# The second layer's injections three steps ahead, with the inputs laid two quarters from the step sizes

## The chip, the core and the metric

The kernel runs on one core of a Trainium2 chip. The metric is the time of one execution on the device in microseconds, from repeated runs of the whole kernel. A core has several engines with an instruction stream each, which meet only at semaphores: TensorE (PE in the profile, with its weight loads as PEld) multiplies matrices and writes into PSUM; VectorE (DVE), ScalarE (ACT) and GpSimd (POOL) work on rows of 128 partitions; SyncE (SP) issues the transfers between memories. All data here are float32.

## The reference

The input x has 8 images of 128 channels, 128 x 128 pixels. A first layer (a dilated convolution, Fourier transforms, a gate) makes an image of the same shape from it; the change doesn't touch it. The second layer is a 3 x 3 convolution, then a small state-space scan on each pixel, a group norm, a SiLU and a residual. The scan reads a pixel's 128 channels as a sequence of 8 tokens of 16 values:

```python
seq = y.reshape(B * H * W, 8, 16)                    # 8 tokens
xz = seq @ in_proj.T;  xi, z = split(xz)             # 32 inner channels each
xc = silu(causal_conv1d(xi))
dt, Bm, Cm = split(xc @ x_proj.T)                    # 1, 16 and 16 values per token
dt = softplus(dt * dt_proj_w + dt_proj_b)            # 32 step sizes
h = exp(dt * A) * h + (dt * xc) * Bm                 # 32 x 16 states, token after token
y_t = sum_over_16_states(h * Cm)
ym = (y + D * xc) * silu(z);   out = ym @ out_proj.T
```

Three quantities matter here: the decay exp(dt * A), made from the step sizes dt; the injection (dt * xc) * Bm, made from the inputs u = dt * xc; and the states h.

## The kernel before

Layer 2 works on 256 blocks of four image rows, so N = 512 pixels each. The state of a block lies on partitions as 16 states x 8 channels. The 32 inner channels are four groups of eight, and a tile of [128, 2, 512] holds two groups (GP = 2). The 8 tokens times two pairs of groups give 16 steps: step s is token s // 2 and pair s % 2.

For each step the kernel does this:

- `spreads` (the matmuls have L800 in the profile) takes two things out of the tile `du` on PE. `du` has four quarters of 32 rows, one for each group. `lay_du` puts the group's step sizes into rows 0 to 7 of its quarter and its inputs u into rows 8 to 15 (SP, 16 transfers a block, L774). A matmul of 16 rows spreads the step sizes over 128 partitions times A (tile `da`), another spreads the inputs (tile `ups`). Which quarter a matmul reads also decides which 32 rows of the PE array it takes up. In one call the kernel spreads `da` of step s + 1 and `ups` of step s + 2, which lie in opposite halves of the rows.
- `exps` (ACT, L805) takes the exponential of `da` in PSUM.
- `inject` (DVE, L815) multiplies `ups` by B's row `bb` into a new tile `h`.
- `decay` (DVE, L831 in PSUM, or L829 into `ah` in steps 4, 7 and 10) multiplies `da` by the state of the token before; `add` (DVE, L839, or POOL, L837 in those three steps) adds it to `h`.
- `weigh` (POOL, L845) multiplies `h` by C's row into `hc`; `collect` (PE, L866) sums over the states into `yps`.

Steps 14 and 15, the last token, need no new state: `last_decay` (DVE, L850) multiplies the decay into an `hc` that `weigh` made from the states of steps 12 and 13. The first and last token's own injections go a shorter way through `end_products` (POOL, L822), `ends_sum` (PE, L856) and `ends_inputs` (DVE, L860).

The order of the instructions on each engine is written out by hand: `step(i, s)` for s from 2 to 11 and then `seam(i)`, which ends block i and begins block i + 1. Work of several blocks is mixed there: the convolution of block i + 3 (L134), the projections of blocks i + 2 (`project_x`, L736 and ACT L738; `project_z`, L745 and ACT L747) and i + 1 (dt, B and C), the output of block i - 1 (`gated` L877, `project_out` L885, and `keep`, which takes its statistics on DVE, L897, and stores it). Each queue works in that order, so an instruction that waits holds what is behind it.

PSUM has room for one `ups` tile, two `da` tiles (which `project_x` and `project_z` also take in turn), one `pm` for all else and one `yps`. So the spread of an `ups` waits until `inject` has read the one before, and the spread of a `da` until the last reader of the one before the last is through. The pool of `h` tiles has six buffers, that of `du` two.

The middle of a step is, on PE, the spreads; on DVE, decay, add and inject:

```python
spreads([(i, s + 1)], [(i, s + 2)])
exps(i, s + 1)
...
if now:
    decay(i, s)
    if s != 4:
        add(i, s)
    inject(i, s + 2)
```

So at the end of step 11 the injections of block i are made up to step 13, and the seam makes those of steps 0 to 3 of the next block.

Of the kernel before, what the change touches and what calls it, by code (L numbers as in the profile page):

```python
# [26 lines left out]
DI = 32  # L27
DS = 16
KC = 4
NG = 4  # L30
# [559 lines left out]
def layer1(ctx, tc, x1, w1, c1, out):  # L590
# [12 lines left out]
    nc = tc.nc  # L603
# [9 lines left out]
    def cf(name):  # L613
        at, n = C1[name]
        return ct[:, at:at + n]
# [21 lines left out]
    taps = cf("taps").rearrange("p (k l) -> p k l", l=L)  # L637
    w_k = wf("conv1d_w").rearrange("p (k d) -> p k d", d=DI)
    with tc.tile_pool(name="l1_prep", bufs=2) as prep:
# [18 lines left out]
        for hf in range(NH):  # L658
            for l in range(L):
                k = hf * L + l  # L660
# [16 lines left out]
    GP = 2  # L677
# [1 line left out]
    wk1 = ctx.enter_context(tc.tile_pool(name="l1_w1", bufs=1))  # L679
    wk2 = ctx.enter_context(tc.tile_pool(name="l1_w2", bufs=2))  # L680
    wk3 = ctx.enter_context(tc.tile_pool(name="l1_w3", bufs=3))
    hp = ctx.enter_context(tc.tile_pool(name="l1_h", bufs=6))
    hcp = ctx.enter_context(tc.tile_pool(name="l1_hc", bufs=7))
    p_u = ctx.enter_context(tc.tile_pool(name="l1_pu", bufs=1, space=PSUM))
    p_a = ctx.enter_context(tc.tile_pool(name="l1_pa", bufs=2, space=PSUM))
# [10 lines left out]
    def live(i):  # L696
        return 0 <= i < nb
# [4 lines left out]
    def load(i):  # L702
        b, r = blocks[i]
        if r % CH == 0:
            lo, hi = max(0, r - 1), min(H, r + CH + 1)
            xin = wk2.tile([P, CH + 2, W], F32, name="xin")
            nc.sync.dma_start(xin[:, :hi - lo, :], x1[b][:, lo:hi, :])
            xins[b, r // CH] = xin, lo
        st8[i]["xin"] = xins[b, r // CH]
# [20 lines left out]
    def pair():  # L730
        return p_a.tile([P, GP, N], F32, name="da")
# [17 lines left out]
    def project_dt(i, hf):  # L749
        d, pool = st8[i], wk2 if hf else wk1  # L750
        ps = misc().rearrange("p a b -> p (a b)")
        nc.tensor.matmul(ps, m_dtf, d["xc"][:, hf, :], start=True, stop=True)  # L752
        d["dt", hf] = pool.tile([P, N], F32, name=f"dt{hf}")
        nc.scalar.activation(d["dt", hf], ps, AF.Softplus, bias=wf("dt_b"))  # L754
# [12 lines left out]

    def lay_du(i, hf):

        d = st8[i]  # L770
        du = wk2.tile([P, LP, N], F32, name="du")
        for q in range(NG):
            for k, v in ((0, d["dt", hf]), (8, d["u", hf])):
                nc.sync.dma_start(du[q * DI + k:q * DI + k + 8], v[q * DI:(q + 1) * DI, :])  # L774
        d["du", hf] = du

    def lay_states(i, hf, k):
# [9 lines left out]
    def spreads(das, upss):  # L787

        todo = []
        for m, name, k0, steps in ((m_a, "da", 0, das), (m_u, "ups", 0, upss)):  # L790
            for i, s in steps:
                if not live(i):
                    continue
                d, t, k = st8[i], s // GP, s % GP
                d[name, s] = pair() if name == "da" else p_u.tile([P, GP, N], F32, name="ups")
                for q in range(GP):
                    a = (k * GP + q) * 32
                    todo.append((d[name, s][:, q], m[a:a + 16, :], d["du", t // LP][a:a + 16, t % LP, :]))
        for o, w, v in todo:
            nc.tensor.matmul(o, w, v, start=True, stop=True)  # L800

    def exps(i, s):
        if live(i):
            da = st8[i]["da", s]
            nc.scalar.activation(da, da, AF.Exp)  # L805

    def state_row(i, name, t):
        return st8[i][name, t // LP][:, t % LP:t % LP + 1, :].broadcast_to([P, GP, N])

    def inject(i, s):  # L810
        if not live(i):
            return
        d = st8[i]
        h = hp.tile([P, GP, N], F32, name="h")
        nc.vector.tensor_mul(h, d["ups", s], state_row(i, "bb", s // GP))  # L815
        d["h", s] = h
# [24 lines left out]
    def weigh(i, s, t):  # L841

        d = st8[i]
        hc = hcp.tile([P, GP, N], F32, name="hc")
        nc.gpsimd.tensor_mul(hc, d["h", s], state_row(i, "cc", t))  # L845
        d["hc", t * GP + s % GP] = hc

    def last_decay(i, s):
        d = st8[i]
        nc.vector.tensor_mul(d["hc", s], d["da", s], d["hc", s])  # L850
# [11 lines left out]
    def collect(i, t):  # L862

        d = st8[i]
        for g in range(NG):
            nc.tensor.matmul(  # L866
                d["yps"][g * DI:(g + 1) * DI], gather[:, t % LP, :], d["hc", GP * t + g // GP][:, g % GP],
                start=False, stop=(t in (3, 6)), skip_group_check=True)

    def skip(i, hf):  # L870
        d = st8[i]
        nc.tensor.matmul(d["yps"], m_d, d["xc"][:, hf, :], start=False, stop=False, skip_group_check=True)  # L872
# [72 lines left out]
    def step(i, s):  # L945

        now, nxt = live(i), live(i + 1)
        if s == 2:
            if live(i + 4):
                load(i + 4)  # L950
            if live(i - 2) and blocks[i - 2][1] + RB == H:
                norm_of(blocks[i - 2][0])
        spreads([(i, s + 1)], [(i, s + 2)])
        exps(i, s + 1)

        if s == 2:
            if nxt:
                project_dt(i + 1, 0)
            if live(i - 1):
                collect(i - 1, 7)  # L960
        elif s == 3:
            if live(i - 1):
                collect(i - 1, 6)
                skip(i - 1, 1)
            if nxt:
                project_bc(i + 1, 0)
        elif s == 4 and nxt:
            project_dt(i + 1, 1)
        elif s == 5:
            if now:  # L970
                ends_sum(i, 0)
            if nxt:
                project_bc(i + 1, 1)
        elif s == 6:
            if now:
                skip(i, 0)
            if live(i - 1):
                project_out(i - 1, 0, 4)
        elif s == 7 and now:
            collect(i, 1)  # L980
        elif s == 8 and live(i - 1):
            project_out(i - 1, 4, 8)
        elif s == 9 and now:
            collect(i, 2)
        elif s == 11 and now:
            collect(i, 3)
        if s in CONV and live(i + 3):
            conv(i + 3, *CONV[s])

        if now:  # L990
            decay(i, s)
            if s != 4:
                add(i, s)
            inject(i, s + 2)
            if s == 5:
                ends_inputs(i, 0)
            if s == 11:
                gated(i, 0)
        if s == 3 and live(i - 1):
            gated(i - 1, 1)  # L1000

        if now:
            if s == 2:
                end_products(i, 0)
            else:
                weigh(i, s - 1, (s - 1) // GP)
            if s == 4:
                add(i, s)
            if s == 7:
                end_products(i, 1)  # L1010
        if s in (3, 4) and nxt:
            inputs(i + 1, s - 3)
        if s == 9 and "active" in fin:
            last_sum()

        if s == 3 and now:
            lay_states(i, 1, 1)
        elif s == 6 and nxt:
            lay_du(i + 1, 0)
            lay_states(i + 1, 0, 0)  # L1020
        elif s == 8 and tails:
            last_load()
        elif s == 10 and nxt:
            lay_states(i + 1, 0, 1)

    def seam(i):


        now, nxt = live(i), live(i + 1)

        def taps(k0, k1):
            if live(i + 3):
                conv(i + 3, k0, k1)

        spreads([(i, 13)], [(i + 1, 0)])
        exps(i, 13)
        if now:
            ends_sum(i, 1)
            decay(i, 12)
            add(i, 12)  # L1040
            weigh(i, 11, 5)
            weigh(i, 12, 7)
        if nxt:
            lay_states(i + 1, 1, 0)
        taps(5, 6)
        if "loaded" in fin:
            last_act()
        if live(i + 2):
            project_x(i + 2)
        if now:  # L1050
            decay(i, 13)
            add(i, 13)
            weigh(i, 13, 7)
        inject(i + 1, 0)
        if live(i + 2):
            project_z(i + 2)
        spreads([(i, 14)], [(i + 1, 1)])
        exps(i, 14)
        if now:
            ends_inputs(i, 1)  # L1060
        inject(i + 1, 1)
        taps(6, 8)
        spreads([(i, 15)], [(i + 1, 2)])
        exps(i, 15)
        if live(i - 1):
            keep(i - 1)
        inject(i + 1, 2)
        if now:
            collect(i, 4)
            last_decay(i, 14)  # L1070
        taps(8, 9)
        if now:
            weigh(i, 12, 6)
            last_decay(i, 15)
        spreads([(i + 1, 2)], [(i + 1, 3)])
        exps(i + 1, 2)
        inject(i + 1, 3)
        if now:
            collect(i, 5)
            weigh(i, 13, 6)  # L1080
        if live(i + 3):
            turn(i + 3)
        if nxt:
            lay_du(i + 1, 1)
# [95 lines left out]
```

## Time and profile before

| | |
|---|---|
| median of 3 runs | 14885.76 us (14885.24 to 14897.25) |
| the profiled execution | 14897.05 us, its span 14895.3 us |
| first `inject` of layer 2 | at 2070.6 us |
| last `inject` of layer 2 | at 14742.5 us |
| one block of layer 2 (from an inject of the seam to the same one of the next block) | 49.23 us |
| in that block: busy PE, DVE, POOL, ACT | 47.74, 46.42, 45.71, 29.00 us |
| DMA engines' busy share in it | 0.66 |
| mean granted TensorE clock | 0.987 |

A timeline line has the start in us, the duration in us, the engine, the line of the kernel, the operation, the tile written and the tiles read with their shapes, and how many instructions of the kind follow each other; in brackets the engine's idle time ahead of it and what ended that. "issue" there means that the profile shows nothing that it waited for. Durations of neighbours on one engine overlap by up to a tenth of a microsecond, so starts are the better measure. A float32 matmul appears as two instructions. A matmul that takes up only some rows of the array can run beside another one in other rows.

### The profile page before, as it was taken

What the parts mean: (1) busy time and instruction counts of PE and PEld (TensorE: products, weight loads), DVE (VectorE), ACT (ScalarE), POOL (GpSimd) and SP (SyncE); (2) the same over time, 40 slices, a digit from 0 to 9 for tenths busy, and PEclk for the clock granted to TensorE, in tenths of its full rate; (3) what the DMA queues carried; (4) which work ended last, traced back from release to release, by engine and by line L of the source; (5) the groups of instructions that cost most, each with busy time, mean ns of one, the idle gap of its engine ahead of it and who ended that gap; (6) DMA issues with size and microseconds to landing.
All of it is one profiled execution on the core that took longest, in us unless ns stands there. A gap on an engine that the chain in (4) does not pass through costs nothing.

```text
span 14895.3 us, 200912 instructions
## 1 busy us (share of the span) xinstructions
PE 14287.1 (96%) x70696; PEld 5588.1 (38%) x70696; DVE 12683.2 (85%) x12417; ACT 8294.9 (56%) x9234; POOL 12983.2 (87%) x7076
## 2 busy tenths in 40 slices
PE   9999999999999999999999999999999999999996
PEld 6677653333333333333333333333333333333331
DVE  3343359999999999999999999999999999999995
ACT  3354355555555555565655555555555555555553
POOL 6666668989999999999999999999999999999996
PEclk9999999999999999999999999999999999999997
DMA  4444456666666666666666666666666666666665
GB/s 136 139 139 122 129 124 117 120 118 121 130 137 134 137 132 136 133 135 134 135 136 133 136 133 137 133 138 131 137 133 136 132 137 133 134 135 135 136 133 140
DMA packets 1091885, 1976.01 MB, mean 133 GB/s; under 512 B 125760, under 2 KB 256832, under 8 KB 1082688
## 3 DMA queue, kind: packets, MB, share of 16 engines
q1 hardware_dynamic: 1090304, 1960.82, 61.0%
q8 instruction: 563, 9.22, 0.3%
q14 instruction: 442, 3.62, 0.1%
q10 hardware_dynamic: 576, 2.35, 0.0%
HBM read 419.16 MB, written 201.33 MB: 42 GB/s over the span
## 4 chain that ended last, share of the span: by engine, by line
PE 72%; DVE 18%; issue 4%; ACT 4%; DMA 1%; POOL 0%; SPq 0%; DVEq 0%; POOLq 0%; ACTq 0%
PE da L800 19%; PE yps L866 9%; PE ups L800 7%; PE pm L134 7%; DVE da L831 6%; PE m L280 4%; DVE h L839 4%; DVE h L815 4%; PE yps L872 4%; PE pm L752 4%; PE pm L885 3%; PE pm L764 3%; DVE hc L850 2%; PE da L745 2%; PE yps L856 2%
## 5 line engine op out<-in xcount | busy, mean ns | idle before, releaser
L845 POOL TENSOR_TENSOR hc<-h,cc 128x1024 f32<-128x1024 f32 x3584 | 8377.2, 2370 | 427.6 <-DVE h L839 408.5
L805 ACT ACTIVATE da<-da 128x1024 f32<-128x1024 f32 x3584 | 3618.7, 1010 | 4193.3 <-PE ups L800 2491.7
L815 DVE TENSOR_TENSOR h<-ups,bb 128x1024 f32<-128x1024 f32 x3584 | 4368.7, 1219 | 690.1 <-PE ups L800 313.9
L800 PE MATMUL da<-du,m_a 16*128 16x512 f32 x14336 | 4068.1, 644 | 140.5 <-DVE hc L850 135.1
L800 PE MATMUL ups<-du,m_u 16*128 16x512 f32 x14336 | 4114.3, 642 | 2.5 <-DVE h L815 1.4
L839 DVE TENSOR_TENSOR h<-da,h 128x1024 f32<-128x1024 f32 x2304 | 2821.2, 1224 | 79.1
L831 DVE TENSOR_TENSOR da<-da,h 128x1024 f32<-128x1024 f32 x2304 | 2820.1, 1224 | 6.8 <-ACT da L805 3.3
L134 PE MATMUL pm<-xin,l_wt 128*128 128x508 f32 (+1 forms) x4608 | 2412.7, 624 | 177.0 <-ACT xr L890 170.2
L837 POOL TENSOR_TENSOR h<-ah,h 128x1024 f32<-128x1024 f32 x768 | 1818.8, 2368 | 451.2 <-DVE ah L829 409.6
L800 PEld LDWEIGHTS da<-du,m_a 16*128 16x128 f32 x14336 | 1078.4, 184 | 2624.6 <-issue 1002.7
L866 PE MATMUL yps<-hc,l_ct 128*32 128x512 f32 x14336 | 1931.7, 611 | 0.0
L134 PEld LDWEIGHTS pm<-xin,l_wt 128*128 128x128 f32 x4608 | 751.7, 189 | 1620.7 <-issue 1396.0
L800 PEld LDWEIGHTS ups<-du,m_u 16*128 16x128 f32 x14336 | 1124.4, 184 | 380.8 <-DVE h L815 298.2
L805 ACT ACT_TABLE_LOAD x774 | 993.0, 1283 | 30.1 <-PE ups L800 1.3
L829 DVE TENSOR_TENSOR ah<-da,h 128x1024 f32<-128x1024 f32 x768 | 933.1, 1215 | 0.0
L759 POOL TENSOR_TENSOR u<-dt,xc 128x512 f32<-128x512 f32 x512 | 656.0, 1281 | 190.2 <-ACT dt L754 190.2
L866 PEld LDWEIGHTS yps<-hc,l_ct 128*32 128x32 f32 x14336 | 283.6, 108 | 1375.1 <-issue 968.6
L754 ACT ACT_TABLE_LOAD x511 | 655.6, 1283 | 29.6 <-PE pm L752 2.1
L822 POOL TENSOR_TENSOR cb<-bb,cc 128x512 f32<-128x512 f32 x512 | 658.3, 1286 | 11.8 <-DMA cc<-bc 11.8
L885 PEld LDWEIGHTS pm<-m_o,ym 128*128 128x128 f32 x4096 | 517.6, 191 | 317.2 <-issue 316.5
L850 DVE TENSOR_TENSOR hc<-da,hc 128x1024 f32<-128x1024 f32 x512 | 600.6, 1215 | 0.9 <-ACT da L805 0.8
L872 PE MATMUL yps<-xc,m_d 128*128 128x512 f32 x1024 | 584.6, 653 | 0.0
(180 smaller groups left out, 14537.5 us busy)
## 6 DMA issues: line engine op xcount, KB each, us to landing
bb<-bc SPq DMA_DIRECT2D x2048, 256.0 KB
cc<-bc SPq DMA_DIRECT2D x2048, 256.0 KB
du<-dt SPq DMA_DIRECT2D x2048, 64.0 KB
du<-u SPq DMA_DIRECT2D x2048, 64.0 KB
xin<-x SPq DMA_DIRECT2D x152, 768.0 KB
xin<-x SPq DMA_DIRECT2D x112, 640.0 KB
gn<-xr SPq DMA_DIRECT2D x256, 256.0 KB
v<-gn SPq DMA_DIRECT2D x256, 256.0 KB
```

Source lines behind the costliest of these rows:

```text
L134: nc.tensor.matmul(out[:, a:b, wa:wb], wt[:, t, :], src[:, r + dy + a - base:r + dy + b - base, wa + dx:wb + dx], start=(n == 0), stop=(n ...
L800: nc.tensor.matmul(o, w, v, start=True, stop=True)
L805: nc.scalar.activation(da, da, AF.Exp)
L815: nc.vector.tensor_mul(h, d["ups", s], state_row(i, "bb", s // GP))
L829: nc.vector.tensor_mul(d["ah"], da, before)
L831: nc.vector.tensor_mul(da, da, before)
L837: nc.gpsimd.tensor_add(h, d["ah"], h)
L839: nc.vector.tensor_add(h, d["da", s], h)
L845: nc.gpsimd.tensor_mul(hc, d["h", s], state_row(i, "cc", t))
L866: nc.tensor.matmul(d["yps"][g * DI:(g + 1) * DI], gather[:, t % LP, :], d["hc", GP * t + g // GP][:, g % GP], start=False, stop=(t in (3, ...
L872: nc.tensor.matmul(d["yps"], m_d, d["xc"][:, hf, :], start=False, stop=False, skip_group_check=True)
L885: nc.tensor.matmul(d["pm"][:, j, :], d["ym", hf][:, j * C:(j + 1) * C], m_of[:, hf, :], start=(hf == 0), stop=(hf == NH - 1))
```

## The change

It does four things in layer 2. `spreads` and `inject` are given `ups` of step s + 3 beside `da` of step s + 1, instead of s + 2; in step 11 that is step 0 of the next block, and the seam then makes steps 1 to 4. The inputs of a group are laid into the quarter two further on than its step sizes, and the `ups` matmuls read them from there. The pool of `h` has seven buffers. In the seam, `keep` stands ahead of `inject` of step 2, `weigh(i, 12, 6)` ahead of the injection that follows, and the injection of step 3 between the two last decays rather than behind both.

```diff
-    hp = ctx.enter_context(tc.tile_pool(name="l1_h", bufs=6))
+    hp = ctx.enter_context(tc.tile_pool(name="l1_h", bufs=7))
...
         for q in range(NG):
-            for k, v in ((0, d["dt", hf]), (8, d["u", hf])):
-                nc.sync.dma_start(du[q * DI + k:q * DI + k + 8], v[q * DI:(q + 1) * DI, :])
+            for k, v, g in ((0, d["dt", hf], q), (8, d["u", hf], (q + GP) % NG)):
+                nc.sync.dma_start(du[q * DI + k:q * DI + k + 8], v[g * DI:(g + 1) * DI, :])
...
                 for q in range(GP):
-                    a = (k * GP + q) * 32
+                    a = (k * GP + q + (GP if name == "ups" else 0)) % NG * 32
...
-        spreads([(i, s + 1)], [(i, s + 2)])
+        ahead = (i, s + 3) if s < 11 else (i + 1, 0)
+        spreads([(i, s + 1)], [ahead])
...
             if s != 4:
                 add(i, s)
-            inject(i, s + 2)
+        inject(*ahead)
+        if now:
...
-        spreads([(i, 13)], [(i + 1, 0)])
+        spreads([(i, 13)], [(i + 1, 1)])
...
-        inject(i + 1, 0)
+        inject(i + 1, 1)
         if live(i + 2):
             project_z(i + 2)
-        spreads([(i, 14)], [(i + 1, 1)])
+        spreads([(i, 14)], [(i + 1, 2)])
         exps(i, 14)
         if now:
             ends_inputs(i, 1)
-        inject(i + 1, 1)
-        taps(6, 8)
-        spreads([(i, 15)], [(i + 1, 2)])
-        exps(i, 15)
         if live(i - 1):
             keep(i - 1)
         inject(i + 1, 2)
+        taps(6, 8)
+        spreads([(i, 15)], [(i + 1, 3)])
+        exps(i, 15)
         if now:
             collect(i, 4)
             last_decay(i, 14)
+            weigh(i, 12, 6)
+        inject(i + 1, 3)
         taps(8, 9)
         if now:
-            weigh(i, 12, 6)
             last_decay(i, 15)
-        spreads([(i + 1, 2)], [(i + 1, 3)])
+        spreads([(i + 1, 2)], [(i + 1, 4)])
         exps(i + 1, 2)
-        inject(i + 1, 3)
+        inject(i + 1, 4)
         if now:
             collect(i, 5)
             weigh(i, 13, 6)
```

## The prediction

> **What bounds the kernel now.** I read the page first: shares by engine, then slices. Layer 2 fills slices 6 to 40, and three engines are nearly full there.
>
> ```profile
> span 14895.3 us, 200912 instructions
> PE 14287.1 (96%) x70696; PEld 5588.1 (38%) x70696; DVE 12683.2 (85%) x12417; ACT 8294.9 (56%) x9234; POOL 12983.2 (87%) x7076
> L815 DVE TENSOR_TENSOR h<-ups,bb 128x1024 f32<-128x1024 f32 x3584 | 4368.7, 1219 | 690.1 <-PE ups L800 313.9 <-issue 311.2 <-POOL hc L845 38.0
> ```
>
> The groups come next. L815 is `inject`, the product with B. It is the only frequent DVE row with much idle time ahead of it: 690.1 us. The timelines say where. One block takes 49.23 us (the inject at 8015.68 us returns at 8064.91). DVE's gaps per block are 0.80, 1.15, 0.16, 0.16 and 0.22 us, sum 2.49, and all stand before an inject. The first three lie in the seam. With x' for step x of the next block, DVE's seam reads add 13, inject 0', ends_inputs, inject 1', bn_stats, inject 2', last decays 14 and 15, inject 3':
>
> ```profile
> 8011.92 1.22 DVE L839 TENSOR_TENSOR h<-da,h 128x1024 f32<-128x1024 f32 x1
> 8013.06 1.21 DVE L815 TENSOR_TENSOR h<-ups,bb 128x1024 f32<-128x1024 f32 x1
> 8014.19 0.69 DVE L860 TENSOR_TENSOR yps<-yps,u 128x512 f32<-128x512 f32 x1
> 8015.68 1.23 DVE L815 TENSOR_TENSOR h<-ups,bb 128x1024 f32<-128x1024 f32 x1 [0.80 <-PE ups L800]
> 8016.82 0.68 DVE L897 BATCH_NORM_STATS2 st<-xr 128x6 f32<-128x512 f32 x1
> 8018.66 1.22 DVE L815 TENSOR_TENSOR h<-ups,bb 128x1024 f32<-128x1024 f32 x1 [1.15 <-issue]
> 8019.80 2.35 DVE L850 TENSOR_TENSOR hc<-da,hc 128x1024 f32<-128x1024 f32 x2
> 8022.30 1.23 DVE L815 TENSOR_TENSOR h<-ups,bb 128x1024 f32<-128x1024 f32 x1 [0.16 <-PE ups L800]
> ```
>
> Each of those injects starts 0.10 to 0.16 us after its spread on PE. PE's timeline of the same stretch:
>
> ```profile
> 8014.90 0.63 PE L800 MATMUL ups<-du,m_u 16*128 16x512 f32 x2
> 8017.91 0.59 PE L800 MATMUL ups<-du,m_u 16*128 16x512 f32 x2
> 8019.43 1.12 PE L134 MATMUL pm<-xin,l_wt 128*128 128x508 f32 x2
> 8021.07 0.70 PE L800 MATMUL da<-du,m_a 16*128 16x512 f32 x2 [0.52 <-DVE hc L850]
> 8021.61 0.59 PE L800 MATMUL ups<-du,m_u 16*128 16x512 f32 x2
> ```
>
> The reader is to see a chain through both engines. The spread of 2' ends at 8018.50; inject 2' runs from 8018.66; last decay 14 from 8019.80; it frees the PSUM buffer that the spread of da 2' needs; PE, free about 8020.5, sits until 8021.07; its group ends at 8022.20 and inject 3' follows at 8022.30. From there DVE runs without a gap to 8042.6. The chain of waits names the same stations.
>
> **What the Trainium skill says.** "PSUM — Partial Sum Buffer", section "Engine vs sequencer instructions": VectorE's queue is strict FIFO, and matmuls start and complete in program order. The trace agrees: the last decays sat behind inject 2' although nothing of theirs was missing. "TensorE: Matmul & The Clock Gate", "Part 3: Packing small matmuls", "The mechanism": weight loads overlap running matmuls only where the row group differs. The trace shows da and ups groups starting 0.01 us apart and done in about 1.07 us (8008.23 to 8009.30), but 2.26 us where ups had to wait (8040.23 to 8042.49). "ScalarE: Activation LUTs", "What ACT_TABLE_LOAD costs", states 1283 ns; the trace has 1.28 us, and the exp after it starts 1.29 us after the load did, so the further drain that the page counts is not seen here. "Perfetto Trace Analysis", "Identifying the Most-Contended Engine": matmul busy share is no measure of PE's limit. The trace agrees: 1.07 against 2.26 us both count as busy.
>
> **The change part by part.** No instruction is added or removed; 14 injects, 14 da groups and 14 ups groups a block remain.
>
> *Edits that cost nothing.* A seventh h buffer is memory alone. `lay_du` issues the same 16 transfers of 64 KB a block in the same SP order from other rows. With ups three ahead, ups and da of a step have the same parity s; without the shift by two quarters they would share row groups, and a group would take about 2.3 us (1.13 + 1.20, the serial case above) instead of 1.07. With the shift they stay apart: 1.07 stays. In steps 2 to 11 DVE, PE, ACT, POOL and SP keep their order; only the index of ups and inject moves on. So the 0.16 and 0.22 us gaps of steps 7 and 10 stay.
>
> *Inputs needed earlier.* The spread of 0' moves from 8008.24 to the group at 8004.28, inject 0' from 8013.06 to 8006.54. In the second half, ups 8' moves from 8037.12 to 8033.59. du's last transfers are issued at 8042.97 (first half, next block) and 8024.19. The DMA activity in 0.5 us slices from 8037 on, then from 8018 on:
>
> ```profile
> DMA  0000302415545555999989999889887881006889
> DMA  9895554123223314959999998988994400000000
> ```
>
> In the first, the engines are empty from 8054.0 to 8055.0, so B's rows are in before inject 0' (8055.77 for that block); du, issued while the share was at most half, was out ten microseconds before its group at 8053.51. In the second they are mostly idle from 8021.5 to 8026 while du is issued, and everything is in by 8034; du precedes the large transfer behind it, so I put it near 8027, six microseconds early. Cost zero; if that cover failed, each microsecond late would cost up to 255 us in all.
>
> *The seam.* DVE's new order is add 13, inject 1', ends_inputs, bn_stats, inject 2', last decay 14, inject 3', last decay 15, inject 4'. The starts, with durations and start-to-start steps of the rows above (inject to next 1.14, last decay 1.17):
> - inject 1' at 8013.06: its spread is PE's group of 8008.23, done at 8009.37. ends_inputs 8014.19, bn_stats 8014.89 to 8015.57.
> - inject 2': its spread is the group of 8014.35, held there as before by the Silu of xc (ACT, ends 8014.15), done 8015.53, so 8015.68. The 0.80 us gap shrinks to 0.1.
> - last decay 14 needs exp 14, and it now stands ahead of inject 3'. On ACT:
>
> ```profile
> 8014.46 1.02 ACT L747 ACTIVATE zs<-da 128x1024 f32<-128x1024 f32 x1 [0.31 <-PE da L745]
> 8015.56 1.28 ACT L805 ACT_TABLE_LOAD   x1
> 8016.85 1.01 ACT L805 ACTIVATE da<-da 128x1024 f32<-128x1024 f32 x1
> ```
>
>  exp 14 ends at 8017.86, whatever DVE does; with 0.1 us to get across, last decay 14 starts at 8017.96, where DVE has sat since 8016.82: a new gap of 1.1 us takes the place of the 1.15.
> - inject 3': spread done 8018.50; DVE free at 8017.96 + 1.17 = 8019.13, ends 8020.35. last decay 15 at 8020.27 (exp 15 was done at 8019.60, POOL's product for it about 8019.0).
> - PE's group da 2' + ups 4': PE is free at 19.43 + 1.05 = 8020.48; da's buffer is free since 8019.2; inject 3' has freed ups's at 8020.35. It starts 8020.48, not 8021.07, and ends 8021.61.
> - inject 4' at 8021.72 (DVE free at 8021.44), where inject 3' stood at 8022.30.
>
> Gain 0.58 us a block, bounded above by PE's 8020.48. The gaps become 0.1 + 1.1 + 0.3 + 0.38 = 1.9 us against 2.49, which fits. What follows moves along: turn on PE starts at 22.6 instead of 23.14, the next group 23.15 instead of 23.72, exp 2' ends 8022.68 for decay 2' at 8022.86. POOL's long run of products ends near 8024.8 and then waits 1.33 us for add 2'; 0.75 of that is left, so POOL is not reached. bn_stats moved forward costs its 0.68 us in a gap.
>
> *The sum.* 255 seams x 0.57 us (a little off for the exp's crossing, which the trace of before doesn't show by itself: 0.05 to 0.25 us; above about 0.15 the margin before 8020.48 is used up, and at 0.25 the gain is 0.48) = 145 us. The profiled execution took 14897.05 us (span 14895.3 and 1.75 around it), so 14752 for it; the median of the runs, 11 us lower, becomes 14741.
>
> **The rivals.**
> - *Nothing comes of it.* The new wait on exp 14 swallows the gain: last decay 14 at 8018.5 instead of 8017.96 makes inject 4' 8022.3 again. For it: ACT's table load stands right ahead. Against it: exp 14's time is read from the trace and its inputs don't move. Time 14886; so would a change that another engine's cycle takes back at once.
> - *Slower.* The same place, beyond its turning point. DVE's queue is in order, so behind last decay 14 stand inject 3', last decay 15 and inject 4', and PE's group of 2' waits for inject 3' with collect, turn and the next block's projections behind it. It decides from a start at 8018.55; each further 0.1 us costs 26 us. A start at 8018.9, as when the Silu pair on ACT comes 0.9 us later, gives 0.35 x 255 = +89: 14975. Against: xc and z are released by adds 12 and 13, which stand unmoved.
> - *Far faster.* If both gaps went in full (1.95 us), 255 x 1.95 = 497: 14389. exp 14 speaks against all of it; half, were the da chain on PE also early, gives 14640.
>
> **How the numbers follow.** Forecast (14710 to 14800) 0.66; part of it (14800 to 14856) 0.09; nothing 0.09; slower 0.12; far faster 0.04. I take 0.2%, 30 us, as what a measurement of this kernel can tell from no change. Faster 0.79, same 0.09, slower 0.12. The range 14705 to 14870 leaves out far faster, slower and half of nothing, about 0.2.
>
> **What would show it.** Right: block period 48.65 us; DVE's seam gaps near 0.1, 1.1 before a last decay (put down to ACT), 0.3; PE's 0.52 us gap before da gone; L815's idle down by some 400 us and L850's up by 280; da and ups still 0.01 us apart. Wrong: an inject waiting for a DMA, ups groups of 2 us everywhere, last decay 14 later than 0.7 us after exp 14, or POOL without idle time after the seam.

## The result, and the profile after

| | before | after |
|---|---|---|
| median of 4 runs | 14890.93 us (14885.24 to 14897.25) | 14715.84 us (14712.15 to 14717.42) |
| profiled execution, its span | 14897.05, 14895.3 us | 14712.15, 14710.4 us |
| one block of layer 2, median of 255 | 49.233 us | 48.557 us |
| one block, mean of 255 (from one `keep` statistic to the next) | 49.315 us | 48.633 us |
| mean granted TensorE clock | 0.987 | 0.988 |

The ratio is 0.9882 (95% interval 0.9865 to 0.9899): 175 us faster. The mean block is 0.682 us shorter; over 255 blocks that is 174 of the 185 us between the two spans. Of the rest, 3 us lie in layer 1, which the change doesn't touch (the first inject of layer 2 stands at 2067.6 instead of 2070.6 us), about 7 us at the entry to layer 2 and 1 us behind the last statistic.

The page of the changed kernel, in the lines that answer to those of before. In this kernel every line number of the scan is one higher, so `inject` is L816 and `last_decay` L851.

```profile
span 14710.4 us, 200914 instructions
PE 14255.2 (97%) x70696; PEld 5593.5 (38%) x70696; DVE 12679.2 (86%) x12417; ACT 8295.0 (56%) x9234; POOL 12984.8 (88%) x7076
L816 DVE TENSOR_TENSOR h<-ups,bb 128x1024 f32<-128x1024 f32 x3584 | 4362.1, 1217 | 239.6 <-PE ups L801 164.6
L851 DVE TENSOR_TENSOR hc<-da,hc 128x1024 f32<-128x1024 f32 x512 | 623.8, 1218 | 281.2 <-ACT da L806 280.3
```

The busy times are what they were: PE 14287.1 to 14255.2, DVE 12683.2 to 12679.2 us. The idle ahead of `inject` fell from 690.1 to 239.6 us, and 281.2 us of a new wait, on the exp, stand ahead of `last_decay`. The difference, 169 us, is nearly the whole change of time. The seam on DVE, from add 13 to decay 2' (a prime marks a step of the next block):

```profile
8018.82 1.22 DVE L840 TENSOR_TENSOR h<-da,h 128x1024 f32<-128x1024 f32 x1
8019.96 1.21 DVE L816 TENSOR_TENSOR h<-ups,bb 128x1024 f32<-128x1024 f32 x1
8021.10 0.69 DVE L861 TENSOR_TENSOR yps<-yps,u 128x512 f32<-128x512 f32 x1
8021.69 0.68 DVE L898 BATCH_NORM_STATS2 st<-xr 128x6 f32<-128x512 f32 x1
8022.54 1.23 DVE L816 TENSOR_TENSOR h<-ups,bb 128x1024 f32<-128x1024 f32 x1 [0.17 <-issue]
8024.86 1.22 DVE L851 TENSOR_TENSOR hc<-da,hc 128x1024 f32<-128x1024 f32 x1 [1.10 <-ACT da L806]
8026.01 1.21 DVE L816 TENSOR_TENSOR h<-ups,bb 128x1024 f32<-128x1024 f32 x1
8027.14 1.21 DVE L851 TENSOR_TENSOR hc<-da,hc 128x1024 f32<-128x1024 f32 x1
8028.58 1.23 DVE L816 TENSOR_TENSOR h<-ups,bb 128x1024 f32<-128x1024 f32 x1 [0.23 <-PE ups L801]
8029.72 1.22 DVE L832 TENSOR_TENSOR da<-da,h 128x1024 f32<-128x1024 f32 x1
```

Three gaps are left: 0.17, 1.10 and 0.23 us, where there were 0.80, 1.15 and 0.16. Last decay 14 now waits for the exp; inject 3' follows it without a gap. PE in the same stretch:

```profile
8024.78 0.59 PE L801 MATMUL ups<-du,m_u 16*128 16x512 f32 x2
8025.30 1.07 PE L867 MATMUL yps<-hc,l_ct 128*32 128x512 f32 x8
8026.30 1.12 PE L134 MATMUL pm<-xin,l_wt 128*128 128x508 f32 x2
8027.35 0.70 PE L801 MATMUL da<-du,m_a 16*128 16x512 f32 x2
8027.89 0.59 PE L801 MATMUL ups<-du,m_u 16*128 16x512 f32 x2
```

The spread of da 2' starts when the convolution ahead of it is through; the 0.52 us in which it waited for last decay 14 are gone. The list of waits (who waited for whom: us in all, times, longest) says the same of all blocks. In the kernel before, PE's weight loads for da waited 343.9 us, 255 times, for the last decays:

```profile
PEld da L800 <- DVE hc L850: 343.9, 255, 2.4
```

In the changed kernel that wait is gone, and the last decays wait for the exp instead:

```profile
DVE hc L851 <- ACT da L806: 280.3, 255, 1.4
PEld da L801 <- DVE hc L851: 1.1, 1, 1.1
PE da L801 <- DVE hc L851: 0.2, 1, 0.2
```

### The profile page after: what moved, and what is told of

The parts are those of the page before. It is cut to its first block, busy times and chain, and to the rows that moved or that the text cites. A ratio compares the mean times of both kernels' runs of the same rounds, so it can differ in the third digit from the quotient of the medians.

```text
span 14710.4 us, 200914 instructions
## 1 busy us (share of the span) xinstructions
PE 14255.2 (97%) x70696; PEld 5593.5 (38%) x70696; DVE 12679.2 (86%) x12417; ACT 8295.0 (56%) x9234; POOL 12984.8 (88%) x7076
## 5 line engine op out<-in xcount | busy, mean ns | idle before, releaser
L816 DVE TENSOR_TENSOR h<-ups,bb 128x1024 f32<-128x1024 f32 x3584 | 4362.1, 1217 | 239.6 <-PE ups L801 164.6
L851 DVE TENSOR_TENSOR hc<-da,hc 128x1024 f32<-128x1024 f32 x512 | 623.8, 1218 | 281.2 <-ACT da L806 280.3
L752 PE MATMUL pm<-xc,m_dt 128*128 128x512 f32 x1024 | 584.7, 653 | 1.5 <-issue 0.8
```

## The experiments

The theory: the gain comes from the order in the seam, because last decay 14 frees the buffer of da 2' early and inject 3' no longer waits behind both last decays; the exp of step 14 then sets the place of last decay 14, with 0.13 us of margin ahead of PE's own time. The rivals: the earlier injections (three steps ahead) carry it, or the moved statistics do. Except where "before" is named, each edit is made to the changed kernel. Ratios are to the kernel before.

**The order alone**, in the kernel before (two ahead, own quarters, six buffers):

```diff
+        if live(i - 1):
+            keep(i - 1)
         inject(i + 1, 1)
...
-        if live(i - 1):
-            keep(i - 1)
-        inject(i + 1, 2)
         if now:
...
             last_decay(i, 14)
+            weigh(i, 12, 6)
+        inject(i + 1, 2)
         taps(8, 9)
         if now:
-            weigh(i, 12, 6)
             last_decay(i, 15)
```

> The seam's new order alone on the kernel before: two steps ahead, inputs in their own quarters, six h buffers; the statistics stand ahead of the injection of step 1, that of step 2 between the two last decays. Theory (the order of the seam is what gained, because PE's group no longer waits for last decay 14 behind a late injection): about 0.62 us of the 0.68 us a block, 14891 - 255 x 0.62 = 14733 us, ratio about 0.989, block 48.6 us. Rival (it is the third step of distance that gained): ratio 0.998 to 1.0, 14860 to 14890 us.

Measured: 14740.62 us (14722.55 to 14743.53), ratio 0.9898 (0.9883 to 0.9913), block 48.642 us. In the median of its blocks, DVE's seam waits 1.06 us for the exp ahead of last decay 14, and 0.21 and 0.27 us ahead of the injects of 1' and 3'.

**All of the change but the order**: three ahead, the laying and the seventh buffer, with the seam in the old order.

> Three steps ahead, the layout and the seventh buffer, with the seam in the order of before (each injection where its predecessor stood). Theory: only the 0.06 us a block that the body gained is left, 14891 - 15 = 14876 us, ratio 0.998 to 1.0, gaps of 0.80, 1.15 and 0.16 us in the seam again. Rival: 14716 us or near it, ratio 0.988.

Measured: 14866.5 us (14853.76 to 14873.6), ratio 0.9984 (0.9977 to 0.9990), block 49.154 us. The order carries some 150 us, the rest of the change some 25; together they make the 175 measured.

**Last decay 14 put behind inject 3'**:

```diff
             collect(i, 4)
-            last_decay(i, 14)
             weigh(i, 12, 6)
         inject(i + 1, 3)
         taps(8, 9)
         if now:
+            last_decay(i, 14)
             last_decay(i, 15)
```

> The changed kernel with last decay 14 put behind the injection of step 3, next to last decay 15. Theory: PE's group for da of step 2 waits for last decay 14 again (a gap of about 0.5 us ahead of it), nearly the whole gain goes: 14716 + 255 x 0.55 = 14856 us, ratio to before 0.996 to 1.0. Rival (the statistics moved forward made the gain): it stays near 14716 us.

Measured: 14868.27 us, ratio 0.9984 (0.9978 to 0.9991), block 49.154 us. In its DVE timeline one gap of 1.77 us stands where the change has 1.10:

```profile
8003.84 1.23 DVE L816 TENSOR_TENSOR h<-ups,bb 128x1024 f32<-128x1024 f32 x1 [1.77 <-PE ups L801]
8004.98 2.35 DVE L851 TENSOR_TENSOR hc<-da,hc 128x1024 f32<-128x1024 f32 x2
8007.49 1.22 DVE L816 TENSOR_TENSOR h<-ups,bb 128x1024 f32<-128x1024 f32 x1 [0.16 <-PE ups L801]
```

And in its list of waits PE's wait for the last decays is back, once in every block:

```profile
PEld da L801 <- DVE hc L851: 347.2, 255, 2.4
PE da L801 <- DVE hc L851: 138.2, 255, 1.4
```

This one line of order is worth 152 us. It takes away nothing that DVE does; it decides when PE gets its buffer. The theory's chain holds.

**The statistics back** behind inject 2':

```diff
-        if live(i - 1):
-            keep(i - 1)
         inject(i + 1, 2)
...
         exps(i, 15)
+        if live(i - 1):
+            keep(i - 1)
         if now:
```

> The changed kernel with the statistics of keep behind the injection of step 2, where they stood before. Theory: they fall into the 1.1 us in which DVE waits for exp 14, so nothing changes: 14716 us within 15. Rival (moving them forward filled the 0.80 us gap and that was the gain): about 0.6 us a block lost, 14870 us.

Measured: 14717.36 us (14714.02 to 14719.01), ratio 0.9884 (0.987 to 0.9899), block 48.556 us: the time of the change. The gaps become 0.76 us ahead of inject 2' and 0.50 ahead of last decay 14, 1.26 us as against 1.27. The 0.68 us of statistics fill one hole or the other, since last decay 14 can't start before the exp either way. So the smaller gap ahead of inject 2', the one that looks like the gain in the timeline, is worth nothing.

**The exp later.** Three small copies on ACT, whose result nothing uses, stand ahead of the exp of step 14:

```diff
+        if live(i + 2):
+            for k in range(3):
+                nc.scalar.copy(idle, st8[i + 2]["yT"][:, k * P:(k + 1) * P])
```

> The changed kernel with three small copies (128 x 128, results unused) on ACT ahead of exp 14, which makes it later by d, about 0.6 us. Theory: last decay 14 stands ahead of the injection of step 3, so the delay passes on less the margin of about 0.13 us: 14716 + 255 x (d - 0.13), 14836 us for d = 0.6, last decay 14 still within 0.1 us of exp 14. Rival (PE's own work sets the end of the seam and DVE has room): under 14750 us.

Measured: 14896.42 us (14891.36 to 14900.05), ratio 1.0001 (0.9992 to 1.001), block 49.219 us. The whole gain is gone. ACT and then DVE in its timeline:

```profile
8009.90 0.95 ACT L1065 COPY idle<-yT 128x128 f32<-128x128 f32 x3
8010.87 1.28 ACT L808 ACT_TABLE_LOAD   x1
8012.16 1.93 ACT L808 ACTIVATE da<-da 128x1024 f32<-128x1024 f32 x2
```

```profile
8013.27 1.23 DVE L853 TENSOR_TENSOR hc<-da,hc 128x1024 f32<-128x1024 f32 x1 [1.88 <-ACT da L808]
```

The wait grew from 1.10 to 1.88 us. Measured from the end of the activation ahead of it, the exp came 0.79 us later, the block grew by 0.66: the first 0.13 us cost nothing (by the whole time, 181 us or 0.71 us a block, it was 0.08). That is about the margin that the prediction had worked out, and it is why the change doesn't gain more: past it, the exp of step 14 sets the end of the seam.

**Six buffers of h instead of seven**, and the same with an unused tile in the room of the seventh, so that the addresses stay as they are:

```diff
-    hp = ctx.enter_context(tc.tile_pool(name="l1_h", bufs=7))
+    hp = ctx.enter_context(tc.tile_pool(name="l1_h", bufs=6))
```

> The changed kernel with six h buffers. Theory: the nearest reuse is the injection of step 4 (at 8028.58 us in the profile) behind the product of POOL with the states of step 12 (ends about 8028.3), so no wait is added: 14716 us within 20. Rival (three steps ahead needs the seventh buffer): DVE waits for POOL in the seam, 0.2 us a block or more, over 14765 us.

> Six h buffers and an unused tile of the seventh's size in its place (zeroed once, about 1 us), so that every later tile lies at the address that it has in the changed kernel. If the 36 us that six buffers cost come from the waits on the buffers: 14752 us again, injections starting 0.1 us or more after their spread in step 7. If they come from where the tiles lie: 14717 us.

Measured: 14751.76 us (14745.27 to 14754.72), ratio 0.9904 (0.9889 to 0.9919), block 48.673 us; with the unused tile 14747.82 us (14745.47 to 14749.83), ratio 0.9905 (0.989 to 0.992), block 48.673 us. The expectation missed: six buffers were expected to be enough, and the loss of the seventh costs 36 us. No run with six buffers comes within 27 us of a run of the change. The second kernel shows that the place in memory isn't the cause. In the timeline of the first, the injections of step 7 and of 4' start 0.05 us later after their spreads than in the change (gaps of 0.10 and 0.23 us there):

```profile
8016.27 1.23 DVE L816 TENSOR_TENSOR h<-ups,bb 128x1024 f32<-128x1024 f32 x1 [0.15 <-issue]
8044.66 1.22 DVE L816 TENSOR_TENSOR h<-ups,bb 128x1024 f32<-128x1024 f32 x1 [0.28 <-issue]
```

Two times 0.05 us is most of the block's 0.116. The label "issue" alone doesn't rule out a buffer that comes free late, since the inject of 2' in the kernel before has it too and waited for its spread. But in the median the product of POOL that read the buffer last ended 3.7 us (step 7) and 0.46 us (4') before these injects start. What differs stands in the instruction records of the traces: with six buffers these two carry a wait for POOL's semaphore, with seven one for PE's alone. In every run's trace, nearly all injects behind a gap start 0.10 to 0.16 us after the end of their spread where they carry POOL's wait, and 0.04 to 0.10 us where they don't. So a wait that was met long before seems to cost some 0.05 us by being there; no run varies it by itself.

**The order and the seventh buffer**, two ahead, in the kernel before:

> The seam's new order with two steps ahead, the inputs in their own quarters, and seven h buffers: the whole change without its third step of distance. If the seventh buffer is what lies between the order alone (14741 us) and the changed kernel (14716 us), as the 36 us lost with six buffers suggest: 14705 to 14720 us, block 48.53 us or so. If the distance is: 14741 us again, block 48.64 us.

Measured: 14730.26 us (14726.05 to 14736.77), ratio 0.9893 (0.9876 to 0.9909), block 48.587 us. With the runs above, all in the new order:

| | six buffers | seven buffers |
|---|---|---|
| two ahead, own quarters | 14740.62 us, block 48.642 | 14730.26 us, block 48.587 |
| three ahead, shifted quarters | 14751.76 us, block 48.673 | 14715.84 us, block 48.557 |

The 25 us that the order leaves to the rest of the change aren't the distance by itself: with six buffers three ahead was no faster than two (11 us slower, within what these runs can tell). The intervals of the ratios overlap, so how the 25 us divide between distance and buffer stays open; the block periods, in one execution each, put it at 0.03 us for the distance with seven buffers.

**Own quarters with three ahead**:

```diff
-            for k, v, g in ((0, d["dt", hf], q), (8, d["u", hf], (q + GP) % NG)):
+            for k, v, g in ((0, d["dt", hf], q), (8, d["u", hf], q)):
...
-                    a = (k * GP + q + (GP if name == "ups" else 0)) % NG * 32
+                    a = (k * GP + q) * 32
```

> The changed kernel with the inputs left in their own quarter, so that da and ups of one step take up the same rows of the array. Theory: each of the 14 groups takes about 2.3 us in place of 1.07; PE's work, 44.0 us a block when nothing waits (49.23 less 1.49 idle and about 3.7 of groups stretched by waits), becomes 61.6, PE alone sets the period and the time is 14716 + 255 x (61.6 - 48.55) = 18040 us (17000 to 19000). Rival (the groups are mostly stretched by waits anyway, so the rows matter little): under 15000 us.

Measured: 17267.76 us, ratio 1.1594 (1.157 to 1.1617), block 57.0 us, clock 0.963. In PE's timeline the two spreads of a group run one after the other:

```profile
8006.49 1.13 PE L801 MATMUL da<-du,m_a 16*128 16x512 f32 x4
8007.45 1.02 PE L801 MATMUL ups<-du,m_u 16*128 16x512 f32 x4
8008.40 1.06 PE L867 MATMUL yps<-hc,l_ct 128*32 128x512 f32 x8
```

From start to start that is 0.96 + 0.95 = 1.91 us a group instead of 1.07. The direction was as expected, the price 1.91 rather than 2.3 us. The 0.84 us don't count fourteen times, though. In the block of the change looked at, eight of the fourteen groups have their two spreads 0.01 us apart; in the other six the spread of ups waits for the inject that frees its tile, in one of them so long that the group is serial already:

```profile
8046.51 1.13 PE L801 MATMUL da<-du,m_a 16*128 16x512 f32 x4
8047.64 1.13 PE L801 MATMUL ups<-du,m_u 16*128 16x512 f32 x4
```

All fourteen groups of a block, each up to the next matmul on PE, take 18.2 us in the change and 26.8 here: 8.6 us more, and the median block is 8.4 longer. The whole time lost 2552 us, some 400 more than 255 such blocks. The clock fits that: in layer 2 it was granted at half for 1031 us, against 140 in the change, and half of the difference, some 450 us, is an estimate of what that cost. The laying is what three ahead can't do without; alone it was not tried.

**Collect 2 moved** from step 9 to step 8, into PE's wait of 0.68 us there:

```diff
-        elif s == 8 and live(i - 1):
-            project_out(i - 1, 4, 8)
-        elif s == 9 and now:
-            collect(i, 2)
+        elif s == 8:
+            if live(i - 1):
+                project_out(i - 1, 4, 8)
+            if now:
+                collect(i, 2)
```

> The changed kernel with the collect of token 2 on PE moved from step 9 to step 8, ahead of the convolution tap that waits 0.68 us for ACT's copy of the output. Theory: PE reaches the group of step 10 about 0.7 us earlier, DVE's gap of 0.23 us ahead of its injection goes: 14716 - 255 x 0.23 = 14657 us, ratio to before 0.984. Rival (the seam takes it back, or the later group of step 9 holds DVE): 14716 us or slower.

Measured: 14714.98 us (14714.36 to 14715.3), ratio 0.988 (0.9865 to 0.9894), block 48.50 us: the median block is 0.06 us shorter in the profiled execution, the mean block 0.02 at most, and the whole time is that of the change. DVE's gap in step 10:

```profile
8008.93 1.23 DVE L816 TENSOR_TENSOR h<-ups,bb 128x1024 f32<-128x1024 f32 x1 [0.17 <-PE ups L801]
```

It shrank from 0.23 to 0.17 us and no more, since there is one `ups` tile: the spread can start only once the inject before has read it, and takes 1.13 us. A PE that is free earlier has nothing to write into.

**Decay 13 into SBUF** (`ah`), added from there on DVE, which would free a `da` buffer 1.2 us earlier for PE; and the same with collect 2 moved and one convolution tap drawn from step 11 to step 10:

```diff
-        if s in ON_POOL:
+        if s in ON_POOL or s == 13:
             d["ah"] = wk1.tile([P, GP, N], F32, name="ah")
             nc.vector.tensor_mul(d["ah"], da, before)
...
+        elif s == 13:
+            nc.vector.tensor_add(h, d["ah"], h)
```

> The changed kernel with the product of decay 13 written to SBUF in place of PSUM (DVE adds from there), so that the PSUM buffer of da 13 is free for project_z one add (1.25 us) earlier. Theory (PE's chain from z to the group of step 2 sets the end of the seam; x before z ends on PE 0.23 us before z starts now): the gap of 0.23 us ahead of z goes, 14716 - 255 x 0.23 = 14657 us, and no more, since PE itself is then full. Rival (DVE's own order sets the end): 14716 us.

> As in the run before it, and PE's work ahead of the seam moved: the collect of token 2 into the gap of step 8, one convolution tap from step 11 to step 10. Theory: PE reaches the seam's first group about 0.45 us earlier, x then waits only for add 12, z starts 0.58 us earlier than in the changed kernel: 14716 - 255 x (0.58 + 0.06) = 14553 us, ratio to before 0.977. Rival (the tap holds up the group of step 11, or exp 14 holds the seam): 14640 us or slower.

Measured: 15763.98 us (15619 to 15886), ratio 1.0555 (1.0504 to 1.0606), clock 0.953; and 15366.98 us (15314 to 15438), ratio 1.0309 (1.0285 to 1.0333), clock 0.962. Both missed by far. DVE and POOL in the first one's timeline:

```profile
3027.79 4.62 DVE L840 TENSOR_TENSOR h<-ah,h 128x1024 f32<-128x1024 f32 x1
```

```profile
3022.04 9.29 POOL L848 TENSOR_TENSOR hc<-h,cc 128x1024 f32<-128x1024 f32 x4
3032.56 4.64 POOL L848 TENSOR_TENSOR hc<-h,cc 128x1024 f32<-128x1024 f32 x2 [1.23 <-DVE h L840]
```

The add took 4.62 us in place of 1.22. It was issued while POOL ran four products without a pause, and ended at 3032.41, 1.1 us after POOL's last one (3022.04 + 9.29 = 3031.33): in this block it hardly ran at all until POOL stopped.

It isn't so in every block. The median over the 256 blocks, 3.165 us, lies between two outcomes. In 115 blocks the add took 1.2 or 1.3 us, and the product of POOL beside it 3.35 us instead of 2.36. In 124 it took 4.2 us or more, in 102 of these 5.8 or 5.9, held past the ends of two of POOL's products until POOL stopped. What decides between them isn't shown: in those 115 and those 102 blocks alike it was issued 0.13 to 0.23 us before the end of a product of POOL. The Trainium skill, "SBUF — State Buffer", section "Who interferes with whom", says that a VectorE instruction with both inputs in SBUF contends with a GpSimd instruction that reads SBUF, and one with at most one SBUF input, outside the two-port modes, doesn't. This agrees: either the add or POOL's product lost time, while every other product and add of DVE in layer 2 on tiles of this size has one operand in PSUM and keeps its 1.22 us.

What followed cost more. A block with an add of 5.8 us or more lasted 57.3 us in the mean, one with an add under 1.4 us 48.8 us. The median of the latter is 48.53 us, 0.03 below the change, so the 0.23 us that the earlier buffer was to bring didn't show there either. In the second kernel 80 blocks had an add of over 4 us, and the median of the undisturbed ones was 48.53 us again.

In PE's timeline of the first kernel, and in the view of stretches (us, then busy time of PE, PEld, DVE, ACT and POOL, the granted clock, the DMA share, GB/s):

```profile
3030.15 1.13 PE L801 MATMUL da<-du,m_a 16*128 16x512 f32 x4
3033.60 2.07 PE L801 MATMUL ups<-du,m_u 16*128 16x512 f32 x4 [2.33 <-DVE h L816]
3035.61 3.66 PE L134 MATMUL pm<-xin,l_wt 128*128 128x508 f32 x4
```

```profile
3026.50:3029.50 3.00, 3.00 (x10) 1.06 (x8) 2.97 (x3) 1.68 (x2) 3.00 (x3) 1.00 0.97 176
3029.50:3033.00 3.50, 1.63 (x8) 0.30 (x4) 3.50 (x2) 3.21 (x4) 2.27 (x2) 0.89 0.66 166
3033.00:3036.00 3.00, 2.40 (x5) 0.90 (x6) 1.97 (x4) 0.66 (x1) 3.00 (x2) 0.50 0.01 3
3036.00:3039.20 3.20, 3.20 (x5) 0.78 (x4) 2.13 (x2) 0.00 (x0) 1.20 (x1) 0.53 0.00 0
```

PE sat idle for 2.33 us. Within that gap, at about 3032.2, its granted clock fell to half, where it stayed until about 3039: the four convolution matmuls took 3.66 us, as against 1.97 in the change, and what stands behind them in the block came late as well.

## Why the prediction was right

14741 us were predicted and 14715.84 measured; the range held it, and the case that came true is the forecast's own.

- *The bound, the chain between DVE and PE in the seam:* right. The order alone gives 0.9898, last decay 14 behind inject 3' gives nearly everything back, and both show it in PE's wait for the last decays.
- *The stations of the seam:* right to 0.04 us. From decay 12 (8008.27 before, 8015.17 after) to last decay 14 the prediction's times give 9.69 us and the trace 9.69; to inject 3' 10.86 and 10.84; to inject 4' 13.45 and 13.41. Inject 3', which held that last place before, stood at 14.03, so the seam gained 0.62 us where 0.58 was put.
- *The new wait on exp 14 and its margin:* right. 1.1 us were predicted and 1.10 found; the prediction's 0.13 us of margin is what the median block showed with the later exp (0.79 later, 0.66 lost). The rivals "nothing comes of it" and "slower" named the true limit; it lies just past where the change stands.
- *The rest of the block:* 0.06 us better than put. Step 7's gap went from 0.16 to 0.10 us, where the prediction let both gaps of steps 7 and 10 stay; step 10's did stay (0.22 to 0.23). With six buffers it is 0.15 us again, so this gain takes the seventh buffer; it takes three ahead too, since with seven buffers and two ahead it stays at 0.16.
- *The seventh buffer, "memory alone":* wrong. Without it the change loses 36 us. The prediction asked only which engine frees a buffer when, and none is late; what six buffers cost lies in how soon an inject starts. This is the mis-sized term of the sum: nothing put, 36 us measured. With six buffers the block is 48.673 us, next to the 48.65 that the prediction gave.
- *The statistics, "0.68 us in a gap":* right that they cost nothing; they bring nothing either.
- *Serial groups without the shift, 2.3 us:* 1.91 measured. The estimate was taken from the group of 8040.23. Its da and ups lie in different rows of the array, as all do in the kernel before; its ups (8041.36) waited for the inject that ended at 8041.31, as PE's weight load there shows. So it was no case of shared rows, and that it came near 1.91 is luck.
- *Inputs needed earlier, POOL:* right. No inject in steady state waits for a DMA. POOL's wait after its long run of products went from 1.33 to 0.65 us, with 0.75 put; it isn't reached, but half of it is used up. The line in POOL's timeline:

```profile
8032.43 2.36 POOL L846 TENSOR_TENSOR hc<-h,cc 128x1024 f32<-128x1024 f32 x1 [0.65 <-DVE h L840]
```

- *The sum:* for the profiled execution 14752 us were predicted and 14712.15 measured. Of these 40 us, 0.682 us a block in place of 0.57 gives 29, and layer 1 and the two ends of layer 2 some 11. The medians differ by 25 only, since the profiled execution of before lay 11 us above the median that the prediction used and that of after 4 us below its own. No version tried was faster than the changed kernel by more than the measurement can tell.

## What to carry to other kernels

Look for the instruction that frees the scarce buffer, not for the engine with the longest gap: ahead of inject 2' a gap of 0.80 us could be closed or left open at no difference, while moving one `last_decay` ahead of one `inject` was worth 152 us. Before counting such a gain, find what the moved instruction will wait for next and how much room it has there: here about 0.1 us, beyond which what ACT lost went into the block (0.66 of 0.79 us). A spare buffer in a rotating pool may be worth having even where no release comes late.

## What the runs showed of the hardware that was not expected

- An add on DVE with both inputs in SBUF, issued beside POOL's products, had two outcomes: 1.2 to 1.3 us in 115 of 256 blocks, with a product of POOL stretched from 2.36 to 3.35 us, or 5.8 to 5.9 us in 102, past the ends of two products until POOL stopped. The page's rule was known; that a held add is passed over by POOL's next products, and that one such instruction costs 1048 us, 7% of the changed kernel's time, was not expected.
- The granted clock of TensorE fell to half after a PE gap of only 2.33 us with light matmuls ahead of it, and stayed there for about 6.8 us (0.89 of full speed in the mean over 3029.5 to 3033, 0.50 and 0.53 up to 3039.2, 1.00 after). The Trainium skill, "TensorE: Matmul & The Clock Gate", "Part 1: The HAM clock gate", says that the clock halves after at least one idle window of some 3.4 us in a free-running count. The length of the slow stretch, two such windows, agrees; the gap here was shorter than one, so a window needn't be wholly idle. It wasn't one case: the clock fell in or just after 19 of this trace's 20 PE gaps of 2.2 to 2.4 us in layer 2, and all 102 of 3.4 us or more. In the run with own quarters it fell 112 times in layer 2, with no PE gap above 1.3 us in the 3.4 us before.
- One buffer fewer in a pool of seven delayed two injects a block by 0.05 us each, with the buffer free 0.46 us or more before, 36 us in the whole time.
